# A graph layer on one core: the search for the edges' windows before the branch on order, fewer passes for the list's words, and another order of work around the list's runs

## The chip, the cores and the metric

The kernel runs on one core of one Trainium2 chip. The metric is the device time in microseconds (us) of one execution. The engines are TensorE (PE, matrix products), VectorE (DVE), ScalarE (ACT), GpSimd (POOL) and SyncE (SP); each works through its own queue of instructions in the order in which they were written into it. All data lies in SBUF (128 partitions), matrix results in PSUM, and everything large in DRAM, moved by DMAs.

## The reference

There are 6250 nodes with 256 features and 100,000 edges, sorted by dst.

```
x_src, x_dst = x[src], x[dst]
e   = relu((x_dst - x_src) @ theta_w.T + theta_b + x_src @ phi_w.T + phi_b)
out = segment_max(e, dst, num_segments=6250)      # 0 where a node has no edge
y   = x + out
return (y - mean(y)) / sqrt(var(y) + 1e-5)        # over the 256 features
```

What depends on the destination alone can leave the maximum. With b = x @ (phi_w - theta_w).T, a node needs max over its edges of b[src], then its own x @ theta_w.T and the biases added, then relu, its x, and the normalisation. So the work is: make b (6250 rows of 256), take a maximum of gathered rows for every node, finish the nodes.

## The kernel before

**Two parts of the nodes.** Nodes 0 to 1129 are part 1. Their edges are cut into 128 chunks of 146 edges, one a partition. GpSimd gathers one row a partition for each of the 146 steps with an indirect DMA (`gather`, L505), in groups of `STEPS` = 8 into a ring of six tiles named `g`; the last of the 19 groups has two steps. The first six groups come from x and are multiplied in place on PE (`x_group`); the 13 others come from `b_rows`, the array of b in DRAM. A step on VectorE (L669, `run`) is g = max(g, min(previous step, cap)), where the cap cuts at a new node. Each finished group of g is written to `maxima`.

Part 2 are the 5120 other nodes, 40 a partition. Each partition owns a stretch of at most `WINDOW` = 800 edges. Where it ends is **searched**: casts of the chunks' ids, a one-hot of partitions (L621, L622), two matmuls (L628), counts (L629) and their sum; `window` (L634 to L635) is the stretch's first edge. Then `gather_run` fetches the 800 destinations and sources of each partition, `dst_w` and `src_w`, from the edge lists in DRAM. `fill_table` (L919 on, VectorE) sorts them into a table of 40 nodes by 36 places.

b's rows are cut into 17 slots. In each of nine batches `choice` and `wanted` pick for each node one edge from each of two slots. These are fetched by PE without any gather: `slot_part` makes a one-hot (L1043 on VectorE or L1045 and L1046 on ScalarE) of the row wanted by each of 1024 nodes and multiplies a slot's rows by it (L1053, `ps_f`, three PSUM buffers), in two halves of 24 matmuls of 512 columns for each of 17 x 5 = 85 parts. VectorE takes the maximum into `acc` (L1064), once a half: 160 times, since the first slot's ten halves are copied by ScalarE. The prediction calls one L1064 a sum.

**The list.** Edges not chosen by any slot become a list. `list_pieces` (a generator; each `yield` is a piece) makes one word an edge from a distance, a node and a source (L1151 to L1165), moves them together in eleven shifts (L1173, L1176), writes them to DRAM (`list_words`), and fetches each partition's share of the list back by three runs (`gather_run` of `dst_w`). VectorE puts the three together (L1195, L1196), and decodes them into `list_src` (L1201 to L1208) and caps. The 248 list steps a partition, 31 groups of eight, are gathered from `b_rows` and go through the same steps (L669) into `maxima_2`.

**The end.** For shares of eight nodes a partition, `rows_of` gathers each node's last maximum from `maxima_1` or `maxima_2` (L505, `g<-maxima,place`), x @ theta_w.T is made on PE (`ps_e`), and VectorE and ScalarE add, normalise (L1260 to L1287) and SP writes the result.

**Order.** GpSimd's order is written by hand: `in_turn` chains every gather and every pause. A pause is a small iota behind a gather, two in the stage of x, none in the stage of b_rows, one in the list's. The others are ordered by the program's scheduler, VectorE's steps with a hint (a step stays behind the gather of the same place of the next group). In the source the order is:

1. group 0 of x, the order check (descents, L574 to L576, summed by L570), and a **branch** (L582, L583) which sorts the edges if they are unsorted; with sorted edges it is passed over. All engines go through it;
2. half of group 1 (four gathers), the search, the two window gathers, the rest of the x groups;
3. the weights' and b's preparation (L700 to L743), `fill_table`, nine times `choice`, `wanted`, `next_group_1(1)`;
4. the list's pieces, with `next_group_1(1)` after pieces 1, 3, 5 up to 13 (counted from 0):

```
    for i, _ in enumerate(list_pieces()):
        if i % 2:
            next_group_1(1)
```

`next_group_1` gathers the next group of part 1, runs the steps of the group before it, places one column of part 1's nodes, and issues one part. When no group is left it issues the part alone. The three runs stand in the list's last piece, so all 13 groups are ahead of them in GpSimd's queue, and 16 parts are issued by then;
5. the list's loop: per group of eight gathers its steps and 2.25 parts (`PACE`);
6. the end's shares.

Of the kernel before, what the change touches and what calls it, by code (L numbers as in the profile page):

```python
# [40 lines left out]
FP = mybir.dt.float32  # L41
I32 = mybir.dt.int32
# [17 lines left out]
TILES = 40  # L60
LIST = 248
WINDOW = 800
R = 36
# [9 lines left out]
TABLE_BITS = 10  # L73
SLOT_BITS = 9
P_BITS = 7
X_RING = 5
STEPS_BITS = 3
OWN_LIST = 288
# [343 lines left out]
def gnn_kernel(ctx: ExitStack, tc: tile.TileContext, x, src, dst, theta_w, theta_b, phi_w, phi_b, out):  # L422
    nc = tc.nc
    N, D = x.shape
    E = src.shape[0]
    T = -(-E // P)
# [6 lines left out]
    T1 = FIRST_STEPS  # L433
# [5 lines left out]
    EDGES = 1 << SORT_BITS  # L439
# [15 lines left out]
    src_list = dram.tile([EDGES], I32, name="src_list")  # L455
    dst_list = dram.tile([EDGES], I32, name="dst_list")
# [23 lines left out]
    def iota(t, step, base, per_partition):  # L480
        return nc.gpsimd.iota(  # L481
            t,
            pattern=[[step, t.shape[1]]],
            base=base,
            channel_multiplier=per_partition,
            allow_small_or_imprecise_dtypes=True,
        )
# [4 lines left out]
    latest = [None]  # L492
# [66 lines left out]
    ident = const.tile([P, P], FP, name="ident")  # L559
# [13 lines left out]
    descents = search.tile([P, T + 1], FP, name="descents")  # L573
    nc.vector.tensor_tensor(descents, dst_i[:, : T + 1], dst_i[:, 1:], op=ALU.is_gt)  # L574
    n_descents = search.tile([P, 1], FP, name="n_descents")
    nc.vector.tensor_reduce(n_descents, descents, AX.X, ALU.add)  # L576
    add_up(n_descents, flags[:, 0:1])
    with (
        tc.tile_pool(name="sort", bufs=1) as sort,
        tc.tile_pool(name="ps_sort", bufs=2, space=PSUM) as ps_sort,  # L580
    ):
        n_unsorted = nc.values_load(flags[0:1, 0:1])  # L582
        with tc.If(n_unsorted > 0):  # L583
            sort_edges(nc, sort, ps_sort, src, dst, src_list, dst_list, ident)
            load_chunks(nc.sync, dst_i, dst_list, T, EDGES)
            load_chunks(nc.sync, dst_1, dst_list, T1, EDGES)
            load_rows(nc.scalar, src_1, src_list, P * T1)
            latest[0] = None
            gather_group(of_x[0], x)
    latest[0] = None  # L590
# [16 lines left out]
    nc.sync.dma_start(maxima_2[0:1, :], lowest_rows[0:1, :D])  # L607
    bad = const.tile([P, 9], FP, name="bad")

    ids = search.tile([P, T + 2], FP, name="ids")
    nc.vector.tensor_copy(ids[:, : T + 1], dst_i[:, 1:])
    iota(ids[:, T + 1 :], 0, 0, T)
    low0 = search.tile([P, 1], FP, name="low0")
    nc.vector.tensor_copy(low0, ids[:, 0:1])
    nc.vector.memset(low0[0:1, :], -1.0)
    last_node = search.tile([P, 1], FP, name="last_node")
    nc.vector.tensor_scalar(last_node, first_node, TILES - 1.0, None, op0=ALU.add)
    hot0 = search.tile([P, P], FP, name="hot0")  # L620
    nc.vector.tensor_scalar(hot0, columns[:, 2, :], low0, None, op0=ALU.is_ge)  # L621
    nc.vector.scalar_tensor_tensor(hot0, columns[:, 2, :], ids[:, T : T + 1], hot0, op0=ALU.is_lt, op1=ALU.mult)  # L622
    counts = search.tile([P, 2], FP, name="counts")
    end = search.tile([P, 1], FP, name="end")
    cut = 2 * D
    for i, (a, b, n) in enumerate(((cut, T + 2, T), (0, cut, cut))):
        pp = misc()
        nc.tensor.matmul(pp[:, : b - a], hot0, ids[:, a:b], start=True, stop=True)  # L628
        nc.vector.tensor_scalar(  # L629
            descents[:, a:n], pp[:, : n - a], last_node, None, op0=ALU.is_le, op1=ALU.add, accum_out=counts[:, i : i + 1]  # L630
        )
        nc.vector.tensor_tensor(end, counts[:, i : i + 1], end if i else pp[:, T + 1 - a : T + 2 - a], op=ALU.add)

    window = const.tile([P, 1], I32, name="window")  # L634
    nc.vector.tensor_scalar(window, end, -float(WINDOW), 0.0, op0=ALU.add, op1=ALU.max)  # L635
    nc.vector.tensor_scalar(bad[:, 0:1], end, float(WINDOW), None, op0=ALU.is_lt)
# [12 lines left out]


# [40 lines left out]
    with (  # L691
# [59 lines left out]
        for k, share in enumerate(shares(4)):  # L751
            n = share[2]
# [387 lines left out]
    def list_pieces():  # L1140
# [50 lines left out]
        list_edges, second, third = dst_w[:, :LIST], dst_w[:, 2 * P : 2 * P + LIST], dst_w[:, 4 * P : 4 * P + LIST]  # L1191
        for i, to in enumerate((list_edges, second, third)):
            gather_run(to, list_words, run_start[:, i : i + 1])
        for i, to in enumerate((second, third)):
            nc.vector.tensor_scalar(mask, edge, ends[:, i + 1 : i + 2], None, op0=ALU.is_ge)  # L1195
            nc.vector.copy_predicated(list_edges, mask, to)  # L1196
# [133 lines left out]
    def fetch_parts(n):  # L1330
        for _ in range(min(n, len(parts))):
            slot_part(*parts.pop(0))

    def next_group_1(n):
        if groups_1:
            i = groups_1.pop(0)
            gathers = gather_group(i, b_rows)
            if i > X_GROUPS:
                run_1(i - 1, gathers)
        if todo:  # L1340
            node_place(todo.pop(0))
        fetch_parts(n)
# [83 lines left out]
```

## Time and profile before

| What | us |
|---|---|
| runs shown: median of three | 777.48 (773.21 to 779.0) |
| the profiled execution, its own time | 778.11 |
| its span in the trace | 776.3 |
| PE busy | 673.0 (87%) |
| VectorE busy | 644.8 (83%) |
| GpSimd busy | 632.5 (81%) |
| ScalarE busy | 527.7 (68%) |
| fetch matmuls (L1053), 2040 | 482.1 |
| gathers from b_rows for the list (L505), 248 | 252.8 |
| steps (L669), 392 | 188.1 |
| gathers from b_rows for part 1 (L505), 98 | 136.1 |

The busy times say little by themselves, since PE, VectorE and GpSimd are each near the top in some stretch. All further readings are made by stretches of the span. In a row of the groups, the numbers behind the bar are the busy time, the mean in ns of one instruction, and the idle time of the engine just before such instructions with what ended it. In a row of the waits they are the total in us, how often, and the longest. In a timeline a row has the start, the duration, the instruction, and in brackets the idle time ahead of it and what released it.

### The profile page before, as it was taken

Reading aid. Unit: us, or ns where it says so; the run is one execution under the profiler, and the core shown is the slowest. Engines: PE = TensorE matmul, PEld = TensorE weight load, DVE = VectorE, ACT = ScalarE, POOL = GpSimd, SP = SyncE. Lnnn points to the kernel's source line nnn. Section 1 sums busy time; section 2 is a strip of 40 time slices with the busy share of each in tenths; the row PEclk is TensorE's granted clock in tenths of the full one; section 3 lists DMA queues with packets and bytes.
Section 4 is the critical chain, followed back from the end, with each engine's and each line's share of the span. In section 5 each row is a group of like instructions: output and inputs, shape, how many; then the busy total and the mean of one; then the engine's idle time right before and its main releaser. Section 6 shows DMA issues by size and latency. Waiting matters only on the chain.

```text
span 776.3 us, 10452 instructions
## 1 busy us (share of the span) xinstructions
PE 673.0 (87%) x3098; PEld 555.0 (71%) x3098; DVE 644.8 (83%) x1199; ACT 527.7 (68%) x734; POOL 632.5 (81%) x872
## 2 busy tenths in 40 slices
PE   0989999367777849999999999999999999999980
PEld 0778888245555637878888888888888888888870
DVE  5499999999888857698888979889797997867881
ACT  0344444289989675778777877877787788626785
POOL 8798887878887855888888888888888888868860
PEclk9999999669989888999999999999999999999995
DMA  8684725695557765977677777767777676745552
GB/s 246 195 281 151 264 84 208 217 339 192 171 151 243 218 214 163 335 210 247 224 248 238 232 231 231 259 206 244 234 241 249 203 244 211 256 170 173 177 181 111
DMA packets 52295, 168.74 MB, mean 217 GB/s; under 512 B 11795, under 2 KB 13377, under 8 KB 44644
## 3 DMA queue, kind: packets, MB, share of 16 engines
q1 hardware_dynamic: 28024, 100.73, 36.5%
q0 software_dynamic: 21664, 59.56, 27.0%
q10 hardware_dynamic: 2540, 7.69, 2.8%
q8 instruction: 27, 0.44, 0.2%
q14 instruction: 40, 0.33, 0.1%
HBM read 103.02 MB, written 65.71 MB: 217 GB/s over the span
## 4 chain that ended last, share of the span: by engine, by line
PE 47%; POOL 13%; DMA 6%; ACT 5%; DVE 5%; issue 4%; DVEq 0%; POOLq 0%; ACTq 0%
PE ps_f L1053 45%; POOL g L505 12%; DMA g<-b_rows,src 3%; ACT x_f L1287 2%; ACT squares L1277 2%; POOL pause L481 1%; DMA dst_w<-list_words,run_start 1%; DVE g L669 1%; DMA maxima<-g 1%; DVE acc L1064 1%; DMA g<-b_rows,list_src 1%; PE ps_e L1248 1%; DMA g<-maxima,place 1%; DVE x_f L1263 1%; PE ps L806 0%
## 5 line engine op out<-in xcount | busy, mean ns | idle before, releaser
L1053 PE MATMUL ps_f<-hot,terms 128*128 128x512 f32 x2040 | 482.1, 397 | 39.5 <-DVE acc L1064 15.6
L1053 PEld LDWEIGHTS ps_f<-hot,terms 128*128 128x128 f32 x2040 | 388.3, 192 | 129.4 <-ACT hot L1046 24.4
L505 POOL DMA_INDIRECT g<-b_rows,list_src x248 | 252.8, 1019 | 55.3 <-issue 38.1
L1045 ACT ACTIVATE hot<-want,minus_row 128x1024 fp32r<-128x1024 f16 x186 | 205.4, 1147 | 109.2 <-PE ps_f L1053 95.1
L1064 DVE TENSOR_TENSOR acc<-acc,ps_f 128x1024 f32<-128x1024 f32 x160 | 194.2, 1217 | 43.0 <-PE ps_f L1053 42.3
L669 DVE SCALAR_TENSOR_TENSOR g<-g,caps 128x256 f32<-128x256 f32 x392 | 188.1, 480 | 16.8 <-DMA g<-b_rows,src 13.0
L1046 ACT ACTIVATE hot<-hot 128x1024 fp32r<-128x1024 f32 x186 | 186.1, 1046 | 0.0
L505 POOL DMA_INDIRECT g<-b_rows,src x98 | 136.1, 1388 | 30.0 <-issue 25.9
L481 POOL IOTA pause<- 128x160 f32 x399 | 122.6, 307 | 5.6
L740 PE MATMUL ps_b<-weights,x_t 128*128 128x256 f32 x388 | 89.0, 383 | 3.5 <-ACT x_t L730 2.6
L740 PEld LDWEIGHTS ps_b<-weights,x_t 128*128 128x128 f32 x388 | 72.0, 190 | 16.0 <-ACT x_t L730 7.0
L505 POOL DMA_INDIRECT g<-in_x_dram,src x48 | 61.2, 1276 | 11.3 <-issue 7.1
L505 POOL DMA_INDIRECT g<-maxima,place x49 | 48.1, 981 | 13.9 <-issue 7.1
L1043 DVE TENSOR_SCALAR hot<-want,row_id 128x1024 fp32r<-128x1024 f16 x69 | 54.7, 793 | 0.3 <-DMA want<-chosen_rows 0.3
L1248 PE MATMUL ps_e<-weights,x_t 128*128 128x256 f32 x192 | 49.1, 383 | 2.3 <-ACT x_t L1243 1.0
L1248 PEld LDWEIGHTS ps_e<-weights,x_t 128*128 128x128 f32 x192 | 32.8, 190 | 6.9 <-ACT x_t L1243 1.8
L743 ACT COPY b_sb<-ps_b 128x512 f32<-128x512 f32 (+1 forms) x25 | 14.4, 578 | 31.6 <-PE ps_b L740 24.1
L743 ACT COPY g<-ps_b 128x512 f32<-128x512 f32 x24 | 14.1, 586 | 29.8 <-PE ps_b L740 28.2
L1287 ACT ACTIVATE x_f<-x_f,r 128x256 f32<-128x256 f32 x49 | 25.3, 589 | 8.6 <-DVE r L1284 8.6
L730 ACT COPY x_t<-ps_xt 128x512 f32<-128x512 f32 (+1 forms) x49 | 26.4, 592 | 5.9 <-PE ps_xt L728 5.8
L1277 ACT ACTIVATE squares<-x_f,r 128x256 bf16<-128x256 f32 x49 | 24.3, 499 | 0.7 <-DVE r L1274 0.7
L1243 ACT COPY x_t<-ps_e 128x512 f32<-128x512 f32 x24 | 13.7, 576 | 15.6 <-PE ps_e L1241 15.5
(256 smaller groups left out, 502.2 us busy)
## 6 DMA issues: line engine op xcount, KB each, us to landing
maxima<-g SPq DMA_DIRECT2D x49, 1024.0 KB
want<-chosen_rows SPq DMA_DIRECT2D x85, 256.0 KB
x_q<-in_x_dram SPq DMA_DIRECT2D x12, 512.0 KB
b_rows<-b_sb ACTq DMA_DIRECT2D x12, 512.0 KB
raw<-b_rows SPq DMA_DIRECT2D x16, 336.0 KB
x_f<-in_x_dram SPq DMA_DIRECT2D x5, 1024.0 KB
out_dram<-x_f SPq DMA_DIRECT2D x5, 1024.0 KB
g<-b_rows,list_src POOLq DMA_INDIRECT x248, 3.5
```

Of the source, the lines that this page charges most:

```text
L481: return nc.gpsimd.iota(t, pattern=[[step, t.shape[1]]], base=base, channel_multiplier=per_partition, allow_small_or_imprecise_dtypes=True,)
L505: in_turn(nc.gpsimd.indirect_dma_start(out=out, out_offset=out_offset, in_=in_, in_offset=in_offset))
L669: one = nc.vector.scalar_tensor_tensor(g[:, k, :], last[part], caps[:, t : t + 1], g[:, k, :], op0=ALU.min, op1=ALU.max)
L740: nc.tensor.matmul(ps[:, h, :], x_t[:, h, k, :], weights[:, k, 0, :], start=(k == 0), stop=(k == KC - 1))
L1043: nc.vector.tensor_scalar(hot[:, b, :], want, row_id[:, b : b + 1], None, op0=ALU.is_equal)
L1045: nc.scalar.activation(hot[:, b, :], want, AF.Abs, bias=minus_row[:, b : b + 1], scale=1.0)
L1046: nc.scalar.activation(hot[:, b, :], hot[:, b, :].bitcast(FP), AF.Relu, bias=1.0, scale=-1.0)
L1053: nc.tensor.matmul(ps[:, w : w + 512], terms[:, part, b, h * P : (h + 1) * P], hot[:, b, w : w + 512], start=(i == 0), stop=(i == n - 1),)
L1064: latest_part[0] = nc.vector.tensor_tensor(to, to, ps, op=ALU.max).ins.name
L1248: nc.tensor.matmul(a[:, i, :], x_t[:, 2 * i + c, :], weights[:, c, 1, :], start=(c == 0), stop=False)
L1277: nc.scalar.activation(squares, x_f[:, k, :], AF.Square, bias=mean[:, k : k + 1], scale=1.0, accum_out=var[:, k : k + 1])
L1287: nc.scalar.activation(x_f[:, k, :], x_f[:, k, :], AF.Identity, bias=mean[:, k : k + 1], scale=inv[:, k : k + 1])
```

## The change

**The search.** It becomes a function, `search_edges`, that also issues the two window gathers. It is called ahead of the branch, and once more inside the branch's body for the case that edges had to be sorted. Group 0 is cut at `EARLY_STEPS` = 6: six gathers, the search with its window gathers, two gathers, the branch, groups 1 to 5 whole. `window` has one clamp more at its upper end. `dst_w` and `src_w` are allocated ahead of the branch.

**The words.** Instead of multiplying the distance and the word by `valid`, and casting, a mask of all ones or zeros is made of `valid` (a multiplication by -1 written as integers), and the finished word is masked by a bitwise and. Three passes over 1440 words a partition go (L1152, L1154, L1163), two come.

**The list's pieces.** There is one `yield` more, behind the three runs. The calls behind the pieces change: `next_group_1` after pieces 3, 7, 13 and 14, and at the other odd pieces a part without a group. So 18 parts instead of 16 are issued ahead of the list's loop, 67 instead of 69 in it, and the last group of part 1 (two gathers) stands behind the three runs in GpSimd's queue, 96 gathers from b_rows instead of 98 ahead of them.

Cut to its core (in `search_edges` the statements are those of before, except as shown):

```diff
+EARLY_STEPS = 6
...
-    gather_group(of_x[0], x)
+    gather_group(of_x[0], x, 0, EARLY_STEPS)
...
     descents, n_descents, add_up(n_descents, flags[:, 0:1])
-    (the branch)
-    gather_group(of_x[1], x, 0, STEPS // 2)
-    (the search)
-        nc.vector.tensor_scalar(window, end, -float(WINDOW), 0.0, op0=ALU.add, op1=ALU.max)
-    early.close()
-    gather_run(dst_w, dst_list, window)
-    gather_run(src_w, src_list, window)
-    gather_group(of_x[1], x, STEPS // 2)
-    for i in of_x[2:]:
+    def search_edges():
+        (the search)
+        nc.vector.tensor_scalar(counts[:, 0:1], end, -float(WINDOW), 0.0, op0=ALU.add, op1=ALU.max)
+        nc.vector.tensor_scalar(window, counts[:, 0:1], float(E - WINDOW), None, op0=ALU.min)
+        nc.vector.tensor_scalar(bad[:, 0:1], end, float(WINDOW), None, op0=ALU.is_lt)
+        gather_run(dst_w, dst_list, window)
+        gather_run(src_w, src_list, window)
+    search_edges()
+    gather_group(of_x[0], x, EARLY_STEPS)
+    (the branch; in its body, last: search_edges())
+    early.close()
+    for i in of_x[1:]:
         gather_group(i, x)
...
-        nc.vector.tensor_tensor(count, order, count, op=ALU.subtract)
-        nc.vector.tensor_tensor(count, count, valid, op=ALU.mult)
-        distance = order.bitcast(I32)
-        nc.vector.tensor_copy(distance, count)
-        nc.vector.tensor_scalar(distance, distance, 20, None, op0=ALU.logical_shift_left)
+        distance, mask = order.bitcast(I32), count.bitcast(I32)
+        nc.vector.tensor_tensor(distance, order, count, op=ALU.subtract)
+        nc.vector.tensor_scalar(mask, valid, -1.0, None, op0=ALU.mult)
+        word = words.bitcast(I32)
         nc.vector.tensor_tensor(
-            count.rearrange(by_node, r=R),
+            word.rearrange(by_node, r=R),
             words.rearrange(by_node, r=R),
             node_part.to_broadcast([P, TILES, R]),
             op=ALU.add,
         )
-        word = words.bitcast(I32)
-        nc.vector.tensor_tensor(word, count, valid, op=ALU.mult)
         done = valid.bitcast(I32)
+        nc.vector.tensor_scalar(distance, distance, 20, None, op0=ALU.logical_shift_left)
         nc.vector.tensor_tensor(done, word, distance, op=ALU.bitwise_or)
+        nc.vector.tensor_tensor(done, done, mask, op=ALU.bitwise_and)
...
             gather_run(to, list_words, run_start[:, i : i + 1])
+        yield
...
     for i, _ in enumerate(list_pieces()):
-        if i % 2:
+        if i in (3, 7, 13, 14):
             next_group_1(1)
+        elif i % 2:
+            fetch_parts(1)
```

More of the change, by code (lines that the diff above doesn't have):

```diff
@@ L571, in add_up @@
         nc.vector.tensor_copy(to, ps)
[L573 to L590, printed above, removed]
-    gather_group(of_x[1], x, 0, STEPS // 2)
     row_id = const.tile([P, KB], FP, name="row_id")
@@ L608, in gnn_kernel @@
     bad = const.tile([P, 9], FP, name="bad")
+    descents = search.tile([P, T + 1], FP, name="descents")
+    nc.vector.tensor_tensor(descents, dst_i[:, : T + 1], dst_i[:, 1:], op=ALU.is_gt)
+    n_descents = search.tile([P, 1], FP, name="n_descents")
+    nc.vector.tensor_reduce(n_descents, descents, AX.X, ALU.add)
+    add_up(n_descents, flags[:, 0:1])
     ids = search.tile([P, T + 2], FP, name="ids")
-    nc.vector.tensor_copy(ids[:, : T + 1], dst_i[:, 1:])
-    iota(ids[:, T + 1 :], 0, 0, T)
     low0 = search.tile([P, 1], FP, name="low0")
-    nc.vector.tensor_copy(low0, ids[:, 0:1])
-    nc.vector.memset(low0[0:1, :], -1.0)
     last_node = search.tile([P, 1], FP, name="last_node")
-    nc.vector.tensor_scalar(last_node, first_node, TILES - 1.0, None, op0=ALU.add)
     hot0 = search.tile([P, P], FP, name="hot0")
-    nc.vector.tensor_scalar(hot0, columns[:, 2, :], low0, None, op0=ALU.is_ge)
-    nc.vector.scalar_tensor_tensor(hot0, columns[:, 2, :], ids[:, T : T + 1], hot0, op0=ALU.is_lt, op1=ALU.mult)
     counts = search.tile([P, 2], FP, name="counts")
     end = search.tile([P, 1], FP, name="end")
[L625 to L632, printed above, removed]
     window = const.tile([P, 1], I32, name="window")
-    nc.vector.tensor_scalar(window, end, -float(WINDOW), 0.0, op0=ALU.add, op1=ALU.max)
-    nc.vector.tensor_scalar(bad[:, 0:1], end, float(WINDOW), None, op0=ALU.is_lt)
-    early.close()
     tables = body.enter_context(ExitStack())
@@ L643, in gnn_kernel @@
     src_w = index.tile([P, WINDOW], I32, name="src_w")
-    gather_run(dst_w, dst_list, window)
-    gather_run(src_w, src_list, window)
-    gather_group(of_x[1], x, STEPS // 2)
-    for i in of_x[2:]:
+    def search_edges():
+        nc.vector.tensor_copy(ids[:, : T + 1], dst_i[:, 1:])
+        iota(ids[:, T + 1 :], 0, 0, T)
+        nc.vector.tensor_copy(low0, ids[:, 0:1])
+        nc.vector.memset(low0[0:1, :], -1.0)
+        nc.vector.tensor_scalar(last_node, first_node, TILES - 1.0, None, op0=ALU.add)
+        nc.vector.tensor_scalar(hot0, columns[:, 2, :], low0, None, op0=ALU.is_ge)
+        nc.vector.scalar_tensor_tensor(hot0, columns[:, 2, :], ids[:, T : T + 1], hot0, op0=ALU.is_lt, op1=ALU.mult)
+        cut = 2 * D
+        for i, (a, b, n) in enumerate(((cut, T + 2, T), (0, cut, cut))):
+            pp = misc()
+            nc.tensor.matmul(pp[:, : b - a], hot0, ids[:, a:b], start=True, stop=True)
+            nc.vector.tensor_scalar(
+                descents[:, a:n], pp[:, : n - a], last_node, None, op0=ALU.is_le, op1=ALU.add, accum_out=counts[:, i : i + 1]
+            )
+            nc.vector.tensor_tensor(end, counts[:, i : i + 1], end if i else pp[:, T + 1 - a : T + 2 - a], op=ALU.add)
+        nc.vector.tensor_scalar(counts[:, 0:1], end, -float(WINDOW), 0.0, op0=ALU.add, op1=ALU.max)
[5 more added lines that the diff above has]
+    gather_group(of_x[0], x, EARLY_STEPS)
+    with (
+        tc.tile_pool(name="sort", bufs=1) as sort,
+        tc.tile_pool(name="ps_sort", bufs=2, space=PSUM) as ps_sort,
+    ):
+        n_unsorted = nc.values_load(flags[0:1, 0:1])
+        with tc.If(n_unsorted > 0):
+            sort_edges(nc, sort, ps_sort, src, dst, src_list, dst_list, ident)
+            load_chunks(nc.sync, dst_i, dst_list, T, EDGES)
+            load_chunks(nc.sync, dst_1, dst_list, T1, EDGES)
+            load_rows(nc.scalar, src_1, src_list, P * T1)
+            latest[0] = None
+            gather_group(of_x[0], x)
+            search_edges()
+    latest[0] = None
+    early.close()
+    for i in of_x[1:]:
         gather_group(i, x)
```

## The prediction

> **What bounds the kernel now.** I read the stretches first: the span cut where the work changes (the branch, the end of the gathers from x, the first run of the list, the first gather of the list, the last fetch). Columns: length, busy time of each engine with its instructions, granted clock, DMA share, GB/s.
>
> ```profile
> 32.90:113.00 80.10, 76.35 (x409) 66.06 (x409) 75.21 (x97) 36.39 (x68) 71.26 (x108) 1.00 0.61 206
> 113.00:279.30 166.30, 121.92 (x498) 93.65 (x497) 151.26 (x314) 122.43 (x181) 136.66 (x101) 0.87 0.66 213
> 279.30:298.70 19.40, 10.34 (x35) 7.88 (x34) 10.11 (x33) 6.59 (x8) 3.87 (x7) 0.74 0.60 206
> 298.70:682.70 384.00, 383.15 (x1691) 315.97 (x1690) 331.23 (x493) 295.69 (x297) 340.60 (x510) 1.00 0.73 237
> ```
>
> From 298.7 to 682.7 TensorE (PE) is busy 383.15 of 384.0 us: the 2040 fetch matmuls (L1053) set the pace, 2.72 us for each of the two sums (L1064) of a part. Before 279.3 PE is not full. There GpSimd (POOL) has no wait of weight. Its gathers from b_rows are the first row of the next fence, its short pauses the second (from the page's groups):
>
> ```profile
> L505 POOL DMA_INDIRECT g<-b_rows,src x98 | 136.1, 1388 | 30.0 <-issue 25.9
> L481 POOL IOTA pause<- 128x160 f32 x399 | 122.6, 307 | 5.6
> ```
>
> 98 gathers of 1.388 us and 0.306 us between them are 166 us, the whole stretch 113.0 to 279.3. So **POOL's queue** decides when the list's three runs go out, and PE decides after that. Between the two lies a hole; these are the waits inside 279 to 299:
>
> ```profile
> POOL g L505 <- DVE list_src L1208: 15.1, 1, 15.1
> PE ps_f L1053 <- DVE acc L1064: 9.1, 1, 9.1
> DVE dst_w L1196 <- DMA dst_w<-list_words,run_start: 5.9, 1, 5.9
> ```
>
> The runs issue at 279.34, their words land at 288.37, VectorE (DVE) works them into list_src by 298.4, and the list's gathers begin at 298.69. PE stands for 9.1 us, because its PSUM buffers are full and DVE's next sum (L1064) is queued behind the instruction that waits for the runs.
>
> **Part 1: the search ahead of the branch.** In the timelines of before (start, duration, instruction):
>
> ```profile
> 14.60 1.35 POOL L481 IOTA order<- 128x1440 f32 x1
> 16.39 0.96 POOL L505 DMA_INDIRECT g<-in_x_dram,src  x1 [0.16 <-issue]
> 17.58 0.81 POOL L481 IOTA work<- 128x800 f32 x1
> 22.69 0.96 POOL L505 DMA_INDIRECT g<-in_x_dram,src  x1 [2.34 <-DMA g<-in_x_dram,src]
> 30.04 0.96 POOL L505 DMA_INDIRECT dst_w<-dst_list,window  x1 [0.56 <-DMA x_q<-in_x_dram]
> ...
> 14.03 2.01 DVE L711 SCALAR_TENSOR_TENSOR bias_terms<-rest,ident,bias 128x256 fp32r<-128x256 f32 x1
> 21.85 0.34 DVE L622 SCALAR_TENSOR_TENSOR hot<-columns,ids,hot 128x128 f32<-128x128 f32 x1
> 26.39 0.15 DVE L635 TENSOR_SCALAR window<-end 128x1 int32<-128x1 f32 x1
> 36.27 0.66 DVE L919 TENSOR_SCALAR wide<-dst_w,first_node 128x800 f32<-128x800 int32 x1 [9.67 <-DMA dst_w<-dst_list,window]
> ```
>
> The changed order puts the search's casts where DVE is idle (9.1 to 11.5), and the one-hot behind L711, which ends at 16.04. One-hot 0.6, carry memset 0.3, then the 4.35 us that lie in before between the end of L622 and the end of L635, and one clamp more at 0.15: window is there at about **21.6** (20 to 23) instead of 26.54. POOL has done its six gathers and its iotas by 17.1 (16.23 where the pause behind `order` ends, and `work` 0.81). So it stands 4.5 us with everything of its queue behind it: two gathers of group 0, the branch, 40 gathers from x, 96 from b_rows. It gets back the 0.56 that dst_w's gather waited in before. All its instructions are the same otherwise, so POOL is **3.9 us later** from here (bounds 1.5 and 6). The branch's own 2.34 I leave as it is.
>
> For DVE the gather goes out at 21.6 instead of 30.04 and lands 6.23 later as in before: 27.8, a gain of 8.4. Here the Trainium skill speaks of the same thing: "DMA: Bandwidth & Descriptors", section "Anatomy of one DMA", gives a GpSimd DMA about 2.0 us and its bytes over 436 GB/s. For 128x800 words of 4 bytes that is an estimate of 2.9 us, a landing at 24.5 and a gain of 11.7. The row has 6.23 for this very tile, so I take the row: 8.4.
>
> What are those 8.4 us worth? The table (fill_table, 36 to 97) starts earlier, and the choices follow. But POOL does not wait for DVE in this stage, so the runs do not come earlier by it; DVE only waits longer for gathers (13.0 us for g<-b_rows in before). And the new order on DVE puts the copies of the weights (L721, done at 23.2 in before) behind the first operation on dst_w: 27.8 + 0.7 + 1.5 = 30. PE's preparation, full from 25 to 140, begins some 4 to 5 us later and ends about 2 later, as ACT's 5.6 us of waits for b_rows<-b_sb absorb some. The first part begins at 163.6, 24 us after, so that this costs nothing; without that cover it costs 2.
>
> **Part 2: fewer passes.** Out go L1152 (1.66), L1154 (0.91) and L1163 (1.66), in come a mask (as L1155, 0.91) and a bitwise and (as L1165, 1.66). DVE saves 1.7 us, hidden since the words were ready at 275.4 and the runs issued at 279.3. POOL gathers faster beside a quieter DVE (1.02 each against the list's stage, 1.39 here): for 1.7 us of a full DVE that is 0.5 us at most. I take **-0.5**.
>
> **Part 3: the groups around the runs.** The last group's two gathers stand behind the runs: 2 x (1.388 + 0.306) = **-3.4** for the runs, free afterwards in POOL's 15.1 us of idle. Sum up to the runs: +3.9 - 0.5 - 3.4 = 0. Issue at 279.3, landing at 288.4, give or take 4.
>
> Then DVE's order. In before, 15 sums of 160 stand ahead of the first operation on the landed words (L1196), and two more 1.25 us of small work behind it; the first of them ended at 290.84 and PE went on. In after, 14 stand ahead, although two parts more are issued before the list's loop, and 2.75 us of steps and small operations lie between the landing and the next sum. So PE goes on 1.5 later and one sum (2.72) further back: **+4.2** for the end of the fetch (682.7), bounds -3 and +8. The low end: after its stop PE took 6.1 us for the next sum (290.9 to 297.0), so a shorter stop could save 3.4 of them; that, and POOL earlier by up to 4. list_src comes within 2 us of where it is now (298.4): 1.5 lost before the sum, and the 2.24 that DVE waited for PE largely gone. POOL needs 248 x 1.517 = 376 us for the list, up to 675, and stays ahead of PE's end. The two early parts bring PE nothing by themselves, because only its total from the hole on counts.
>
> **The tail.** In before the last eight steps (L669) follow the last sum at once and the last block of maxima_2 is written from 688.6; POOL then stands until it landed:
>
> ```profile
> 688.14 0.48 DVE L669 SCALAR_TENSOR_TENSOR g<-g,caps 128x256 f32<-128x256 f32 x1
> 694.16 0.95 POOL L505 DMA_INDIRECT g<-maxima,place  x1 [6.17 <-DVE x_f L1263]
> ```
>
> In after sixteen steps follow the last sum, the last eight between the first share's operations, which wait for PE at a pitch of 2.4: the last step comes about 5.8 later against the end of the fetch. Forty gathers of 1.4 hang on it (694.2 to 749.6). Their consumers run some 2 us behind them (a late pair lags 4.9 us its gather, the shortest 2.9), so 3.8 of the 5.8 come through; some steps finish earlier and free the end's mixed work of DVE and ScalarE. I take **+2** (bounds 0 and 5.8).
>
> **Sum.** Against the profiled execution, 778.11 (span 776.3): +4.2 + 2 = +6.2, **784.3**. The median of the runs shown is 777.48, 0.6 less: **783.7**. About 1% (7.8 us) is what a measurement of this kernel can tell from no change: below 769.7 is faster, above 785.3 slower.
>
> **The rivals.**
> *Head start carried through, faster.* DVE is 8.4 us ahead at 28 and the first part starts earlier. If POOL's gathers between 33 and 279 are slowed by DVE's heavy passes (36 gathers from x took 79.5 us, where their undisturbed pitch of 1.73 makes 62), and these passes now lie elsewhere, POOL may win back its 3.9 and some 4 more; if the hole of 9.1 then closes because PE still has the two early parts, -9 to -10 in all: **768**. Against it: the same passes still run beside POOL, only 8 us sooner, and the sums' places on DVE are worse. 12%.
> *POOL's stop and the tail at full price, slower.* One mechanism: everything passes in order through POOL, from the stop at window. It decides once the stop is over 6 us (window at 23 or later, if the search's matmuls or the branch are slower there); then +5.5 for the runs, less 3.4, +4.2 at the hole and all of the tail's slip less the consumers' 2: +10, **788** (up to 797). For it: nothing in POOL's queue waits for DVE, so nothing gives the stop back. 18%.
> *Nothing reaches the end.* The landing might come late enough that DVE's steps fit into the wait, PE's stop ends as now, and the consumers' lag hides the slipped step: within 2 us, **778**. For it: DVE has 5.9 us of idle there. Against: more steps stand between the landing and the next sum. 13%.
>
> **How the numbers follow.** My forecast has 57%, with 779 to 789 as its own range, two fifths of it over the bound of slower. Slower: 0.23 + 0.18 = 0.41, rounded to 0.40. Faster: 0.12. Same: 0.48. The range of 8 in 10 reaches down to 770, where most of the faster case is cut off, and up to 793, where a third of the slower one is.
>
> **What would show it.** POOL idle 3 to 6 us ahead of dst_w's gather, issue near 21.6; landing near 27.8; the last gather from x about 4 later than 110; the first run within 4 us of 279.3; PE's stop as long as now or longer, its end at 684 to 690; last step 12 us after the last sum. It is wrong if the runs issue before 274, if the fetch ends before 681, or if the first gather from maxima_2 keeps its 11.5 us from the end of the fetch.

## The result, and the profile after

The changed kernel takes 784.58 us (median of four runs, 783.28 to 786.94), the kernel before 777.45 beside it. The ratio is 1.0104, with a 95% interval of 1.0055 to 1.0152; every ratio in this document compares the fast runs of both kernels, and slow ones came up only on the two chips of the last four experiments. The profiled execution of the changed kernel took 783.51, its span is 781.7, 5.4 longer than before's 776.3. The forecast for it was 784.3. The sum is right; its two terms are not, as the stretches show. These are the changed kernel's, cut at the same events as those of before (last gather from x, first run of the list, first gather of the list, start of the last sum):

```profile
35.80:115.80 80.00, 78.49 (x423) 67.72 (x422) 78.24 (x109) 38.26 (x71) 71.07 (x109) 1.00 0.63 211
115.80:275.40 159.60, 119.51 (x481) 92.71 (x479) 138.47 (x294) 116.52 (x173) 130.67 (x99) 0.87 0.65 212
275.40:291.00 15.60, 6.66 (x22) 5.37 (x23) 9.38 (x24) 6.91 (x8) 5.75 (x9) 0.67 0.56 180
291.00:683.10 392.10, 388.80 (x1717) 320.62 (x1715) 330.01 (x489) 304.45 (x306) 344.09 (x517) 1.00 0.73 234
683.10:781.70 98.60, 70.11 (x418) 62.55 (x416) 63.82 (x221) 62.01 (x175) 50.23 (x80) 0.89 0.48 165
```

Before's last stretch, which the prediction does not show:

```profile
682.70:776.30 93.60, 68.33 (x418) 61.62 (x416) 61.55 (x213) 61.66 (x175) 54.98 (x88) 0.90 0.47 161
```

The list begins at 291.0, 7.7 us earlier than before. Nothing of this is left at 683.1, where the last sum starts (682.7 before): the fourth stretch is 392.1 long instead of 384.0. It holds 142 of the 160 sums instead of 140 (5.4 us at 2.72), and PE has 3.3 us of gaps in it instead of 0.85. After the last sum, 98.6 us remain, where before had 93.6. So the changed kernel gains 8 us up to the list, gives 8 back up to the end of the fetch, and loses 5 at the end.

The front, in the changed kernel's timelines of POOL and VectorE:

```profile
19.22 0.95 POOL L506 DMA_INDIRECT dst_w<-dst_list,window  x1 [1.86 <-SPq L643]
115.78 1.68 POOL L506 DMA_INDIRECT g<-b_rows,src  x1 [0.72 <-DVE at L997]
275.45 0.94 POOL L506 DMA_INDIRECT dst_w<-list_words,run_start  x1 [0.30 <-issue]
...
27.04 0.64 DVE L925 TENSOR_SCALAR wide<-dst_w,first_node 128x800 f32<-128x800 int32 x1 [3.91 <-DMA dst_w<-dst_list,window]
280.38 0.44 DVE L1202 COPY_PREDICATED dst_w<-words,dst_w 128x248 int32<-128x248 int32 x1 [8.00 <-DMA dst_w<-list_words,run_start]
```

POOL stands 1.86 us at the window and not 4.5. The window gather's data come 7.8 after its issue (6.2 in before). The gathers from b_rows begin 2.7 later than before's 113.07, yet the first run goes out 3.9 sooner than before's 279.34: two gathers fewer stand ahead of it, and the 96 left come at a pitch of 1.663 ((275.45 - 115.78) / 96) against 1.697 ((279.34 - 113.07) / 98). The words of the runs arrive 4.9 after the first run, where before needed 9.0.

The end, in the timelines of VectorE and POOL:

```profile
683.08 1.22 DVE L1070 TENSOR_TENSOR acc<-acc,ps_f 128x1024 f32<-128x1024 f32 x1 [1.50 <-PE ps_f L1059]
...
695.00 0.48 DVE L675 SCALAR_TENSOR_TENSOR g<-g,caps 128x256 f32<-128x256 f32 x1
...
700.09 0.95 POOL L506 DMA_INDIRECT g<-maxima,place  x1 [20.86 <-DMA maxima<-g]
```

The list's last step is 11.9 after the start of the last sum (5.5 in before), and POOL, which has nothing to do for 20.9 us, begins the gathers from maxima_2 17.0 after it (11.5 in before).

### The profile page after: what moved, and what is told of

The parts are those of the page before. It is cut to its first block, busy times and chain, and to the rows that moved or that the text cites. A ratio compares the mean times of both kernels' runs of the same rounds, so it can differ in the third digit from the quotient of the medians.

```text
span 781.7 us, 10444 instructions
## 1 busy us (share of the span) xinstructions
PE 675.7 (86%) x3098; PEld 557.9 (71%) x3098; DVE 641.6 (82%) x1197; ACT 531.9 (68%) x738; POOL 628.3 (80%) x872
## 4 chain that ended last, share of the span: by engine, by line
PE 49%; DMA 10%; POOL 8%; ACT 7%; DVE 5%; issue 3%; DVEq 0%; POOLq 0%; ACTq 0%
PE ps_f L1059 48%; POOL g L506 7%; DMA g<-b_rows,src 7%; ACT squares L1283 2%; ACT x_f L1293 2%; DMA want<-chosen_rows 2%; DVE g L675 1%; DMA g<-maxima,place 1%; ACT hot L1051 1%; DVE x_f L1269 1%; DVE acc L1070 1%; ACT x_t L1249 1%; DVE g L1266 0%; DMA maxima<-g 0%; DMA dst_w<-list_words,run_start 0%
## 5 line engine op out<-in xcount | busy, mean ns | idle before, releaser
L1070 DVE TENSOR_TENSOR acc<-acc,ps_f 128x1024 f32<-128x1024 f32 x160 | 194.1, 1216 | 50.5 <-PE ps_f L1059 49.8
L1052 ACT ACTIVATE hot<-hot 128x1024 fp32r<-128x1024 f32 x188 | 188.1, 1045 | 0.0
L506 POOL DMA_INDIRECT g<-b_rows,src x98 | 131.5, 1342 | 29.9 <-issue 25.2
L506 POOL DMA_INDIRECT g<-in_x_dram,src x48 | 62.7, 1306 | 11.5 <-issue 6.8
L506 POOL DMA_INDIRECT g<-maxima,place x49 | 48.3, 986 | 28.7 <-DMA maxima<-g 20.9
L1049 DVE TENSOR_SCALAR hot<-want,row_id 128x1024 fp32r<-128x1024 f16 x67 | 52.3, 780 | 5.0 <-DMA want<-chosen_rows 5.0
```

Of the source, the lines that this page charges most:

```text
L506: in_turn(nc.gpsimd.indirect_dma_start(out=out, out_offset=out_offset, in_=in_, in_offset=in_offset))
L1049: nc.vector.tensor_scalar(hot[:, b, :], want, row_id[:, b : b + 1], None, op0=ALU.is_equal)
L1052: nc.scalar.activation(hot[:, b, :], hot[:, b, :].bitcast(FP), AF.Relu, bias=1.0, scale=-1.0)
L1070: latest_part[0] = nc.vector.tensor_tensor(to, to, ps, op=ALU.max).ins.name
```

## The experiments

Twelve runs were made. In the first eight the kernel before took 776.9 to 777.13 us beside them. In the last four (`before_sums_behind` and the three with the second and third part together) it took 824.5 to 826.5, the same program on other chips, so their times are not set beside the others', only their ratios.

Two theories stood at the start. A: the loss is the end's, and follows from the number of parts left for the list's loop. B: it is made ahead of the list, by POOL's stop and PE's place. Both turned out too simple. C, D and E, which the expectations below state, were formed after the first four runs.

### after_pace218: the changed kernel, parts spread over the whole loop

```diff
-PACE = 2.25
+PACE = 2.18
```

> The changed kernel with PACE = 2.18 instead of 2.25, so that the 67 parts left for the list's loop are spread over all its 31 groups. Theory A (the loss is the end's: with 2.25 the parts run out one group too soon, and sixteen steps instead of eight are chained behind the last sum): the last step of the list comes about 6 us after the start of the last sum as in before (12 in the changed kernel), the first gather from maxima_2 about 11.5 us after it (17 in the changed kernel), and the time falls by 5 us from the changed kernel's, to 778 to 780. Theory B (the loss is made before the list's loop, by POOL's stop and by PE that stands one sum further back, and the end merely follows): the time stays at 783 to 787. Both: end of the fetch within 2 us of the changed kernel's.

Measured 777.74 us, ratio to before 1.0024 (1.0007 to 1.0041). The end is as in before: in this kernel's timelines of VectorE and POOL, eight steps follow the last sum, the last of them 5.5 after its start.

```profile
686.54 1.22 DVE L1070 TENSOR_TENSOR acc<-acc,ps_f 128x1024 f32<-128x1024 f32 x1 [1.50 <-PE ps_f L1059]
692.02 0.48 DVE L675 SCALAR_TENSOR_TENSOR g<-g,caps 128x256 f32<-128x256 f32 x1
...
697.11 1.07 POOL L506 DMA_INDIRECT g<-maxima,place  x1 [13.55 <-DVE g L1266]
```

Why the parts matter: in `run`, each step of the list is put behind the last part issued so far. The loop has 31 turns. With 69 parts and 2.25 a turn, two parts are still to be issued when the steps of the last group but one are written. With 67 parts all are issued by then, and sixteen steps instead of eight stand behind the last sum. With 2.18, 65 of 67 are issued there. The fetch itself ended 3.4 later than in the changed kernel's profile, as the window gather went out 3.3 later, at 22.53, in this execution and all of POOL's queue with it (the last section shows what stood ahead of it), so the end alone is worth the 98.6 - 92.5 = 6.1 us after the last sum.

### before_pace231: the end's slip put into the kernel before

```diff
-PACE = 2.25
+PACE = 2.31
```

> The kernel before with PACE = 2.31 and nothing else: its 69 parts run out one group sooner, so that sixteen steps follow the last sum as in the changed kernel. Theory A: the first gather from maxima_2 slips by 5 to 6 us against the last sum and the time rises by 5 us, to 781 to 784. Theory B: within 2 us of before.

Measured 780.49, ratio 1.0036 (1.0024 to 1.0048), 3.4 us. In the trace the last sum starts at 682.1, as before, and POOL waits:

```profile
699.10 0.96 POOL L505 DMA_INDIRECT g<-maxima,place  x1 [10.78 <-issue]
```

That is 17.0 after the last sum, the changed kernel's value, and the span behind the last sum is 98.2. The step is confirmed, with a price of 3.4 by the runs and 4.6 in the trace.

### before_search_early, before_words, before_new_pieces: each part alone

The first is the changed kernel with the old words and the old pieces, the other two are the kernel before with the one part.

> The kernel before with the first part alone: the search and its two window gathers ahead of the branch; words and pieces as in before. Theory C (the search ahead of the branch moves VectorE's order: fewer of PE's sums stand ahead of the first operation on the list's words, 13 where before has 16, so PE is further back when the list's loop begins): the end of the fetch is 5 to 8 us later than before's 682.7 although the runs go out no later, and the time is 782 to 786. Theory D (the fewer passes carry the loss of the two parts together): 776 to 779 here.

Measured 779.82, ratio 1.0044 (1.0027 to 1.0062): 2.9 us slower, between what D said and what C said.

> The kernel before with the second part alone (fewer passes for the list's words). Theory C: no loss; in VectorE's order 18 sums stand ahead of the first operation on the list's words (16 in before), so the fetch may end up to 5 us sooner: 772 to 778. Theory D: 781 or more.

Measured 769.28, ratio 0.9896 (0.9863 to 0.9929): 7.6 us faster, more than C said and the opposite of D.

> The kernel before with the third part alone (one yield more behind the runs, next_group_1 after pieces 3, 7, 13 and 14, single parts at the other odd pieces). Theory A: it carries the whole loss, the end's 5 us and, without the earlier front, perhaps up to 4 more for PE's place one sum further back: 782 to 787. Theory B: the loss is the search's, so 776 to 779 here. The list's gathers should start some 3 us sooner than in before, as two gathers stand behind the runs.

Measured 772.05, ratio 0.9938 (0.9912 to 0.9964): 5.1 us faster. A had this part carry the whole loss. The list's gathers start at 289.5, 9 us sooner and not 3.

In these three traces the sums (L1064 or L1070) begin alike, but end at very different times. The row has the shortest, median and longest duration in ns, then the start of the first and of the last sum; the order is search, words, pieces:

```profile
L1070 DVE TENSOR_TENSOR acc<-acc,ps_f x160: 1152/1215/1236, 216.9 to 685.6; 128x1024 f32<-128x1024 f32 x160
```
```profile
L1064 DVE TENSOR_TENSOR acc<-acc,ps_f x160: 1200/1214/1222, 218.5 to 674.2; 128x1024 f32<-128x1024 f32 x160
```
```profile
L1064 DVE TENSOR_TENSOR acc<-acc,ps_f x160: 1196/1214/1261, 215.2 to 670.6; 128x1024 f32<-128x1024 f32 x160
```

So the search ends the fetch 2.9 later than before's 682.7, the words 8.5 sooner, the pieces 12.1 sooner (of which the end takes 5 back). Most of what the words and the pieces gain shows as a shorter stop of PE around the runs. Between 276 and 300 PE waits 11.6 us for sums in before (two waits, the longer is the 9.1 of the prediction), 8.0 with the search alone, but with the words alone and with the pieces alone only:

```profile
PE ps_f L1053 <- DVE acc L1064: 2.1, 1, 2.1
```
```profile
PE ps_f L1053 <- DVE acc L1064: 1.5, 1, 1.5
```

In these two, 18 sums stand ahead of the first operation on the list's words, and 16 in before.

### after_old_pieces: the changed kernel with the third part undone

The list's pieces and the loop around them are those of before.

> The changed kernel with the third part undone: the list's pieces and the loop around them as in before (16 parts ahead of the list's loop, 98 gathers ahead of the runs); the search ahead of the branch and the fewer passes stay. Theory A: the end is as in before (eight steps behind the last sum), and the earlier start of the list (some 4 us, since POOL has two gathers more ahead of the runs than in the changed kernel) reaches the end of the fetch at most in part: 773 to 778. Theory B (POOL's stop costs): 780 or more.

Measured 784.23, ratio 1.0094 (1.0061 to 1.0126). The last sum starts at 688.4, 5.7 later than in before. The words gained 7.6 us by themselves, the search cost 2.9, the two together cost 7.1: the parts do not add. Theory A's 773 to 778 is out, and B's range is met. Something that the search does takes the gain of the others away.

What it does begins ahead of PE's first sums. The list's first long passes on VectorE (1440 words a partition) start at 166.3 in the changed kernel and at 174.0 in before, so most of the head start is still there. But beside these passes POOL's gathers from b_rows are slow: up to 3.8 us each, where the eight ahead of them took 0.94 to 1.38. In before that begins with gather 41, in the changed kernel with gather 34. POOL's timelines, before and then the changed kernel:

```profile
172.96 1.60 POOL L505 DMA_INDIRECT g<-b_rows,src  x1 [0.16 <-issue]
178.04 3.79 POOL L505 DMA_INDIRECT g<-b_rows,src  x1 [0.31 <-issue]
```
```profile
170.31 3.80 POOL L506 DMA_INDIRECT g<-b_rows,src  x1 [0.30 <-DVE g L675]
185.83 2.91 POOL L506 DMA_INDIRECT g<-b_rows,src  x1 [0.16 <-issue]
```

The 3.8 us beside the longest pass (3.1 us) come 7.7 sooner in the changed kernel, as the passes do. The first row and the last are the same gather, the 41st, which comes 12.9 us later there. Gather 65 is still 7.7 later (234.2 against 226.4), and only at gather 89 are the two within 1 us. With the search alone gather 41 is 11.1 later, with the words or the pieces alone within 0.2.

VectorE's steps then wait for these gathers between 213 and 246, where VectorE moves the list's words, works part 1's steps and PE's first sums. These are the waits there, first of before, second of the kernel with the words alone, third of the changed kernel:

```profile
DVE g L669 <- DMA g<-b_rows,src: 1.6, 2, 0.9
```
```profile
DVE g L669 <- DMA g<-b_rows,src: 2.7, 3, 1.1
```
```profile
DVE g L675 <- DMA g<-b_rows,src: 10.3, 6, 3.9
```

In every kernel with the search ahead of the branch VectorE stands 8.5 to 10.3 us there for gathers from b_rows (9.2 with the old pieces; 8.5 with the search alone; 8.6 in the experiment below; 8.5 with PACE 2.18, where all comes some 5 us later and the stretch is 218 to 251). In the others of the first eight runs and in before it is 1.3 to 3.2. The sums queued behind a waiting step wait with it: the seventh starts at 246.4 in the changed kernel and at 239.3 in before. So the head start on VectorE is turned into a wait.

### after_sums_ahead and before_sums_behind: the place of the sums in VectorE's order

Theory C says that what PE has done when the list begins is set by how many sums stand ahead of the first operation on the list's words in VectorE's instruction order. The scheduler's orders differ: 16 in before, 18 with the words alone, 18 with the pieces alone, 13 with the search alone, 12 with search and words, 14 with all three. The last sums start at 682.7, 674.2, 670.6, 685.6, 688.4 and 683.1. That goes together roughly (two sums are 5.4 us, and 16 and 14 ended 0.4 apart), and it is no proof. Two hints were therefore put on this order. In the changed kernel:

```diff
+            one = nc.vector.copy_predicated(list_edges, mask, to)
+            if i == 0:
+                behind_in_order(one, sums[17], "sums ahead of the runs")
```

> The changed kernel, all three parts and PACE 2.25, with one hint on VectorE's order: the first operation on the list's words stays behind the eighteenth sum (in the changed kernel 14 sums are ahead of it). Theory C: PE is four sums (10.9 us) further at that place; the list's start may slip by some us, as the last two gathers now come ahead of it, but the fetch ends 5 to 11 us sooner than the changed kernel's 683, and the time falls to 774 to 780, the end's slip still in it. Theory E (PE is held by something else that the early search does, such as its later preparation or POOL's later gathers): PE does no better, the hint only delays the list, and the time is 784 or more.

Measured 782.95, ratio 1.0100 (1.0062 to 1.0139). The last sum starts 3.3 sooner than in the changed kernel:

```profile
L1071 DVE TENSOR_TENSOR acc<-acc,ps_f x160: 1205/1215/1222, 215.8 to 679.8; 128x1024 f32<-128x1024 f32 x160
```

That is the way C said, with less than its 5 to 11, and the time cannot be told from the changed kernel's 784.58. VectorE's waits for gathers are still there (8.6 us in 213 to 246): the four sums stand ahead of the list's words now, but still behind steps that wait for gathers. The third part alone has 18 sums ahead too, and its last sum starts at 670.6, 9.2 sooner than here; at the seventh sum it is 5.9 ahead already (238.8 against 244.6). The place in the order is the smaller share.

In the kernel before, the reverse:

```diff
+                for late in sums[12:]:
+                    behind_in_order(late, one.ins.name, "sums behind the runs")
```

> The kernel before, search and words and pieces untouched, with one hint on VectorE's order: the sums from the thirteenth on stay behind the first operation on the list's words, so that 12 sums are ahead of it and not 16, which is the place they have where the first two parts of the change are made together. Theory C (the place of the sums in VectorE's order sets where PE is when the list begins): the fetch ends later than before's 682.7 by up to 4 x 2.72 us = 10.9, 686 to 692, and the time is 781 to 788, with no search moved at all. Theory E (the early search costs by PE's later preparation or POOL's later gathers): within 2 us of before.

Ratio 1.0037 (1.0010 to 1.0063), 3 us: slower, as C said, but again less than the 4 to 11 expected; the interval, 0.8 to 5.2 us, does not shut out the 2 us that E allowed.

### before_new_pieces_pace218: the third part without its price

```diff
-PACE = 2.25
+PACE = 2.18
```

in the kernel with the third part alone.

> The kernel before with the third part alone, and PACE = 2.18, so that eight steps and not sixteen follow the last sum. If the end's slip and the gain ahead of it are separate terms, the time falls by 3 to 5 us from that of the third part alone (772.05): 767 to 769. If PE is held back by fewer parts in each turn of the loop, it stays at 772 or rises.

Measured 766.4, ratio 0.9870 (0.9854 to 0.9887). The last sum starts at 670.3 (670.6 with 2.25), and 93.1 us follow it instead of 98.7. The two terms are separate, and without the price at the end the third part gains 1.3%.

### Second and third part together

Without the search, with PACE = 2.18, and once more on another chip:

> The kernel before with the second and third part (fewer passes, new pieces) and PACE = 2.18; the search stays behind the branch. By theory C (16 sums ahead of the first operation on the list's words, 18 ahead of the second, and the runs early): fetch end 666 to 672, and with eight steps behind the last sum 763 to 768. If the gains of the two parts do not add, as they move the same order, it lies at 766 to 769 like the better of each alone.

> The same kernel as before_words_pieces_pace218 (second and third part, PACE = 2.18, search behind the branch), since on the chip of that run the kernel before took 826 us and not 777, which leaves its interval at 0.968 to 0.990. Beside the changed kernel with PACE = 2.18 (777.74, ratio 1.0024) it differs by the first part alone. Theory C (the early search costs the place of the sums): fetch end 666 to 672, ratio 0.980 to 0.988. If the early search costs only its own loss of the run by itself (ratio 1.0044), the ratio is 0.996 to 1.000.

Ratios 0.9786 (0.9675 to 0.9898) and 0.9827 (0.9754 to 0.9900). Beside the changed kernel with 2.18 (1.0024) this differs by the first part alone, which therefore costs some 2% there and not the 0.4% of the run by itself, if a ratio carries over from one chip to another; the intervals (up to 0.990, from 1.0007) do not meet. Whether it beats the third part alone with 2.18 (0.9870) the intervals leave open. 16 sums stand ahead of the first operation on the list's words here, as in before, and 18 ahead of the second: the count at the first alone does not tell the time.

With three parts left over and issued behind the list's last steps:

```diff
-PACE = 2.25
+PACE = 2.09
...
-    assert not parts
     run(2, g_before, STEPS, caps_2, LIST - STEPS, maxima_2t[LIST // STEPS - 1])
+    fetch_parts(len(parts))
```

> As the kernel with the second and third part, but with PACE = 2.09 and the three parts that are left over issued behind the list's last steps, so that the last block of maxima_2 is written while PE still fetches (four sums behind the last step in VectorE's order). If the wait of POOL for maxima_2 at the end holds up the end, the first gather from maxima_2 comes within 5 us of the last sum's start instead of 11 to 17, and the time falls a further 3 to 8 us, to 757 to 764. If the end is bound by VectorE and ScalarE, it stays within 2 us of the kernel with PACE = 2.18.

Ratio 0.9867 (0.9790 to 0.9944): no gain over 2.18 that can be told. In its trace the list's last step starts 8.2 ahead of the last sum, and no gather behind that sum has POOL waiting for as much as 1 us. So in this kernel that wait was not what held up the end.

## Why the prediction was right or wrong

**The sum (784.3 against 783.51)** was right by luck: its two terms were missed by opposite amounts. The fetch's end was put at +4.2 and measured +0.4, the end behind it at +2 and measured +5.0.

**POOL's stop** was put at 4.5 us; it was 1.86 in the profiled execution and 5.27 in that of the same front with PACE 2.18. The step that failed is the start of the one-hot "behind L711, which ends at 16.04": in the changed order that instruction can end at 13.75. The row that was read has 2.01 us for it, and the changed kernel 0.48. From the end of the one-hot to the end of `window` it was as worked out, 4.46 against 4.35 + 0.15. (The terms written down add up to 21.4, not 21.6.)

**The runs** were to go out at 279.3. They went out at 275.45, just inside the 4 us that were given. POOL began at b_rows 2.7 later, where 3.9 was worked out, and the two gathers moved were worth the 3.4. The term mis-sized was the gathers' relief: 0.5 was taken, the pitch of 1.663 against 1.697 is worth 3.2 over 96 gathers. What brings the relief is not settled: the pitch is 1.64 to 1.66 in the kernels with the early search and 1.66 to 1.70 in before and the others of the first eight runs.

**The landing** was carried over as 9.0 after the first run; it took 4.9. That is 4.1 us, beside the 3.9 of the earlier issue, of which 7.7 reached the list's start. What stood beside the runs differs: while they were under way in before, the DMA queue fed by SyncE moved 2.17 MB (b's rows for the slots, maxima, wanted rows), and 0.52 MB in the changed kernel. Seven more traces of the first eight runs say the same: 1.4 to 2.2 MB with landings of 7.2 to 9.8, and at most 0.5 MB with 4.2 to 4.9. A longer landing also leaves more time for other transfers, and no run moved them alone. For the window gather the same choice of the row held better: 7.8 against the row's 6.23, and against the estimate of 2.9 that follows from the Trainium skill ("DMA: Bandwidth & Descriptors", "Anatomy of one DMA").

**PE one sum further back** was a miscount: PE was two sums further back. Not 15 but 16 sums stand ahead of the first operation on the landed words in before, and 14 in the changed kernel. These are the sums up to that operation, of before and of the changed kernel (length, VectorE's busy time with them and their number):

```profile
0.00:288.37 288.37, 19.18 (x16) 0.92 0.65 213
```
```profile
0.00:280.38 280.38, 16.87 (x14) 0.92 0.65 211
```

PE had done 340 fetch matmuls when it stopped in before and 316 in the changed kernel, and 24 are one part, two sums. With that count the term would have been +6.9. PE's stop itself was as long as before, as said:

```profile
PE ps_f L1059 <- DVE acc L1070: 9.3, 1, 9.3
```

It ended at 284.35, 6.5 sooner than before's 290.9: 8 for the runs and their landing, less the 1.5 of small work, which came as worked out. The two sums take 5.4 of that. Another 3.3 go in three gaps of PE between 300 and 319: one behind a load of x_f (1.39), two for ScalarE's one-hots (1.18 and 0.73). I had taken PE as full from 298.7 on, as it nearly was in before (0.85 of gaps up to 340). By these numbers the fetch should end 1.35 later than before (5.4 + 3.3 - 0.85 - 6.5); it ended 0.4 later, and the 0.9 between I have not traced.

**What the step said of the two early parts** ("bring PE nothing by themselves") holds in the changed kernel only. Alone, the third part brought the fetch's end forward by 12.1 us, with 18 sums ahead of the list's words. The second part, put at -0.5 with its passes hidden, brought 7.6 us alone, also with 18 sums ahead. And "DVE only waits longer for gathers" is what happened to the head start, but it was not free: it brought VectorE's long passes to earlier gathers, POOL fell behind there, and the sums behind the waiting steps came later. By the traces that is how the search took away the gain of the two other parts, and it was not in the sum.

**The end** was mis-sized: sixteen steps behind the last sum, and 5.5 us later for the first gather from maxima_2, came as worked out (5.8). But of them 5.0 came through in the changed kernel, not 2; the runs with PACE 2.31 and 2.18 give 3.4 and up to 6.8. The consumers' lag of 2 us, which I set against it, hid little.

**The rivals.** Of the head start carried through, the first half happened in part: POOL had won back its later start by the runs. But PE's stop did not close, and PE was two sums back. POOL's stop at full price did not happen: POOL was ahead at the runs. The third, that nothing reaches the end, is out by the end's 5 us. Of the signs named, POOL's idle time, the issue near 21.6 (19.22) and the fetch's end from 684 on (683.1) were missed; the landing near 27.8 (27.0), the first run and the last step came.

**What stays open.** That the search ahead of the branch costs 0.4% alone, and far more beside the other two parts, is shown. That POOL's gathers come later under VectorE's earlier passes, and that VectorE waits for them, is seen in each trace with the early search. Of the 12.5 us by which the changed kernel ends the fetch later than the third part alone, the hint that gave it the same 18 sums ahead brought back 3.3. That the other 9.2 are the later gathers and the waits behind them is read from the traces; no run moved the passes or the gathers alone.

## What to carry to other kernels

An engine that is brought forward past the producer it depends on only waits; if its work also slows that producer, it waits longer, and if its queue holds another engine's work, that engine waits too. So price a head start by what the next producer in line delivers, and look at what is queued behind the wait. Count that queue in the trace: one sum miscounted was 2.7 us here. When work is moved out of a paced loop, set the pace anew; here two parts fewer at the same pace put eight steps more behind the last sum, for 5 us. Test the parts of a change one by one: of three, two gained 1.0% and 0.6% alone, and the third, a loss of 0.4% alone, took both gains away.

## What the runs showed of the hardware

Indirect gathers from b_rows, issued by GpSimd, took 0.94 to 1.38 us each in the last eight ahead of VectorE's long passes (128x1440, 0.9 to 3.1 us each) and up to 3.8 beside them. Where the passes started 7.7 us sooner, so did the gather of 3.8 us beside the longest of them (170.3 instead of 178.0).

Small VectorE instructions stood beside GpSimd's train of iotas. In the changed kernel the cast of `pick` (128x128), `bias_terms` and the one-hot were over by 14.5, before the large iota `order` began at 15.04. In the kernel with PACE 2.18, whose front is the same program, the first two came a microsecond later, since VectorE had the biases ahead of them 1.3 later (12.69 instead of 11.39), and stood until the iotas were over. First the changed kernel's rows, then the other's:

```profile
13.13 0.22 DVE L720 CAST pick<-pick_one 128x128 fp32r<-128x128 f32 x1
13.27 0.48 DVE L717 SCALAR_TENSOR_TENSOR bias_terms<-rest,ident,bias 128x256 fp32r<-128x256 f32 x1
```
```profile
14.31 3.03 DVE L720 CAST pick<-pick_one 128x128 fp32r<-128x128 f32 x1
14.44 2.91 DVE L717 SCALAR_TENSOR_TENSOR bias_terms<-rest,ident,bias 128x256 fp32r<-128x256 f32 x1
...
16.44 0.82 POOL L482 IOTA work<- 128x800 f32 x1
22.53 0.95 POOL L506 DMA_INDIRECT dst_w<-dst_list,window  x1 [5.27 <-DVE window L630]
```

The two ended at 17.35, with the iota `work` at 17.26. With the search alone it was the one-hot (L618) that stood, 3.12 us instead of 0.16, up to 17.15, with `work` over at 17.06. In before the same two instructions took 2.14 and 2.01, up to 16.04, with `order` over at 15.95: that is the row on which the prediction built. So one front has two outcomes: the window gather at 19.0 to 19.2 in three traces, and at 22.3 to 22.5 in the two where a small instruction fell into the iotas. That the iotas are what holds it is read from these ends alone; no run moved an iota to see.
